# Diagonals of B through DRAM and the skip term on TensorE, in the scan part of a two-layer kernel

## The chip, the cores and the metric

The kernel runs on one core of one Trainium2 chip, in one launch, in float32. The metric is device time in microseconds (us) of the execution. The median of three runs is 18559.42 us (18539.3 to 18562.05).

## The reference

The input x is (8, 128, 128, 128): 8 images of 128 channels. Two layers are applied, each to the group-normalised x, with a residual. Layer 0 mixes a Fourier branch, a channel attention and grouped convolutions; the change doesn't touch it. Layer 1 is a selective scan over the pixels of an image, seen as a sequence of 16,384 tokens. Cut to what matters:

```python
xs, z = split(u @ W_in)                          # 256 + 256 channels
xc = silu(causal_conv4(xs) + conv_b)
dt, Bm, Cm = split(xc @ W_xproj)                 # 8, 16, 16
delta = softplus(dt @ W_dt + b_dt)
# for every token t, channel d (256), state n (16):
h[d, n] = exp(delta[d] * A[d, n]) * h[d, n] + delta[d] * xc[d] * Bm[n]
y[d] = sum_n h[d, n] * Cm[n]
y = (y + xc * D_param) * silu(z)                 # skip term, gate
out = y @ W_out
```

## The kernel before, in words

Parts a to d make layer 0 and write the image x1 to DRAM (X1). The last part, "e", is the scan, lines 1017 to 1390. Nearly all its engine instructions are issued through a helper, InOrder (line 180), which keeps each engine's instructions in program order; so the profile gives them line 180, and they are told apart by their tiles. DMAs on SP aren't held in that order: the scheduler places them.

The tokens are cut into 256 chunks of T = 512 (32 per image). A chunk is worked in 16 steps (ST). A step n has a half h of the channels, a pair mp of state indices and a k, and covers 128 partitions (32 channels x 4 state groups) and two state indices:

- **decay** (ACT): dA = exp(dlrep * A), two 128x512 activations, issued three steps ahead (LEAD). dlrep is delta spread over the partitions; it goes to DRAM (dld) and comes back by four DMAs per half.
- **product** (PE): hb, the term delta * xc * B, 32 matmuls of 64 rows by 32 columns, one step ahead. The moving operand, bd, holds B on the diagonal of 64x64 blocks; the stationary one, duT, is the transposed delta * xc. So the matmul with a diagonal broadcasts B over channels. hb has two PSUM buffers of two banks each.
- **scan** (DVE): two tensor_tensor_scan, reading dA from SBUF and hb from PSUM, writing hs.
- **weigh** (POOL): hc = hs * C (crep, from DRAM by DMA: cd, then four DMAs per pair).
- **add** (PE): matmuls with a 0/1 matrix (gath) that sum hc into y in PSUM, for one half of the channels over 8 steps.
- **keep_state** (ACT): the last column of hs is kept for the next chunk.

Beside this, the list `beside` says which other work is issued at which of the 16 steps, and for which chunk relative to the present one: norm of the input (u<-xin), the convolution as four matmuls per half (e_xc), its activation (xc), the gate (e_z, sz), xproj (e_x, dbl), step_sizes (e_dt) and its softplus (dl), drive on POOL (du = dl * xc), its transposes (e_t, duT), turn_b (four transposes of B, e_bt), keep_b (bt, a copy of B to SBUF), the final projection (e_o) and the residual.

What the change touches:

- **diagonals** (DVE) and **more_diagonals** (ACT): bd is made from a constant (same) and the transposed B. Pair mp = 0 takes four DVE products, pair 1 two DVE products and 16 small ACT activations, spread over steps 11 to 15 and 0 to 1.
- **skip** (DVE, steps 11 and 3): yt = xc * D_param + y, reading y from PSUM. **gated** (POOL, steps 12 and 4): yt = yt * sz.
- **step_sizes_act** (step 7): softplus, dld to DRAM, the four dlrep loads of half 0, the four crep loads of pair 1, the four dlrep loads of half 1.
- Buffers: xin 2, xc 3, bd 2, dlrep 2, crep 3. The four tags bank0 to bank3 are one PSUM bank each: bank1 is shared by half 1 of e_xc, e_z and e_dt and by e_t and e_o; bank2 is e_bt's and bank3 is y's.

Every DMA of SP and ACT takes the next of eight semaphores in turn and so waits until the DMA eight before it has landed.

## Time and profile before

| | us |
|---|---|
| median of three runs | 18559.42 |
| profiled execution, its own time | 18481.4 |
| its span, first to last instruction | 18479.6 |
| scan part: first and last scan start | 6617.5 and 18451.9 |
| busy over the span: PE, DVE, ACT, POOL | 16503.3, 14244.2, 12009.6, 13090.9 |
| mean granted TensorE clock | 0.958 |

| scan part, mean of one (ns) | |
|---|---|
| scan hs, DVE, 128x512, with state | 1269 |
| hc product, POOL, 128x1024 | 2377 |
| dA activation, ACT, 128x512 | 714 |
| table load, ACT | 1283 |
| residual acc, DVE, 128x512 | 1156 |

How to read it: busy time is the union of an engine's instruction spans. Ends of matmuls are modelled, and matmuls overlap, so the distance from one group's start to the next one's says more of the pace than a mean. A wait is put down to the event that came last. "issue" stands for a wait in which nothing that the profile shows was missing. Idle time of an engine that is not the bound costs nothing. The scan part is periodic, so it is read per chunk, from a window in its middle.

### The profile page before, as it was taken

Reading aid. Unit: us, or ns where it says so; the run is one execution under the profiler, and the core shown is the slowest. Engines: PE = TensorE matmul, PEld = TensorE weight load, DVE = VectorE, ACT = ScalarE, POOL = GpSimd, SP = SyncE. Lnnn points to the kernel's source line nnn. Section 1 sums busy time; section 2 is a strip of 40 time slices with the busy share of each in tenths; the row PEclk is TensorE's granted clock in tenths of the full one; section 3 lists DMA queues with packets and bytes.
Section 4 is the critical chain, followed back from the end, with each engine's and each line's share of the span. In section 5 each row is a group of like instructions: output and inputs, shape, how many; then the busy total and the mean of one; then the engine's idle time right before and its main releaser. Section 6 shows DMA issues by size and latency. Waiting matters only on the chain.

```text
span 18479.6 us, 790974 instructions
## 1 busy us (share of the span) xinstructions
PE 16503.3 (89%) x353336; PEld 9529.9 (52%) x353336; DVE 14244.2 (77%) x15987; ACT 12009.6 (65%) x26077; POOL 13090.9 (71%) x7572
## 2 busy tenths in 40 slices
PE   7789988888888889999999999999999999999998
PEld 5566665566555544444444444444444444444444
DVE  5544544334444479999999999999999999999999
ACT  4443434334233358778778878888888878887887
POOL 3333334444222269999999999999999989998998
PEclk8889999988999999999999999999999999999999
DMA  9963337777776654444454445444544454445443
GB/s 375 371 235 89 96 106 248 240 230 218 207 204 192 186 139 100 103 96 100 97 105 101 100 96 108 99 99 98 106 98 99 100 103 100 99 98 105 98 98 88
DMA packets 2434566, 2601.34 MB, mean 141 GB/s; under 512 B 1221965, under 2 KB 1624013, under 8 KB 2396866
## 3 DMA queue, kind: packets, MB, share of 16 engines
q1 hardware_dynamic: 1730850, 2206.28, 43.9%
q10 hardware_dynamic: 679840, 277.32, 7.1%
q0 software_dynamic: 20480, 67.13, 1.1%
q8 instruction: 2783, 45.60, 1.1%
q14 instruction: 613, 5.02, 0.1%
HBM read 1715.23 MB, written 834.93 MB: 138 GB/s over the span
## 4 chain that ended last, share of the span: by engine, by line
PE 56%; DVE 22%; DMA 8%; issue 7%; ACT 6%; POOL 1%; SPq 1%; DVEq 0%; ACTq 0%; POOLq 0%
DVE hs L180 15%; PE hb L180 14%; PE y L180 8%; PE c_mm L180 6%; PE e_xc L180 4%; DVE bd L180 3%; PE e_z L180 3%; PE e_x L180 3%; PE d_b L180 2%; PE a_mm L180 2%; DMA d_of<-OFL 2%; PE c_gram L180 2%; PE d_p L180 2%; DMA X<-d_x 2%; ACT L180 2%
## 5 line engine op out<-in xcount | busy, mean ns | idle before, releaser
L180 POOL TENSOR_TENSOR hc<-hs,crep 128x1024 f32<-128x1024 f32 x4096 | 9653.4, 2377 | 982.4 <-DVE hs L180 858.1
L180 DVE TENSOR_TENSOR_SCAN hs<-dA,state,hb 128x512 f32<-128x512 f32 x7936 | 9611.4, 1269 | 558.2 <-PE hb L180 418.8
L180 PEld LDWEIGHTS hb<-bd,duT 64*32 64x32 f32 x262144 | 3727.5, 106 | 3971.3 <-issue 2808.4
L180 PE MATMUL hb<-bd,duT 64*32 64x128 f32 x262144 | 4919.3, 275 | 798.9 <-issue 417.8
L180 ACT ACTIVATE dA<-dlrep,A 128x512 f32<-128x512 f32 x8192 | 5443.8, 714 | 59.6 <-DMA dlrep<-dld 51.6
L180 PE MATMUL e_xc<-u,wf 128*128 128x512 f32 x4096 | 2263.9, 646 | 34.1 <-DVE A L1046 20.8
L180 PE MATMUL y<-hc,gath 128*32 128x512 f32 x16384 | 2053.4, 601 | 32.5 <-issue 31.2
L180 ACT COPY state<-hs 128x2 f32<-128x2 f32 x4096 | 775.9, 189 | 1676.2 <-DVE hs L180 1649.5
L180 ACT ACT_TABLE_LOAD x1057 | 1356.1, 1283 | 75.0 <-PE e_dt L180 40.1
L180 PE MATMUL c_mm<-src,taps 32*32 32x512 f32 x32768 | 1211.5, 626 | 191.8 <-issue 158.7
L180 DVE COPY vst<-c_mm 128x512 f32<-128x512 f32 x1024 | 685.0, 689 | 717.4 <-PE c_mm L180 620.6
L180 ACT ACTIVATE bd<-same,bt 128x64 f32<-128x64 f32 x4096 | 1054.0, 339 | 0.8 <-PE hb L180 0.8
L180 DVE TENSOR_TENSOR bd<-same,e_bt 128x512 f32<-128x512 f32 x1536 | 1036.7, 675 | 0.0
L180 PEld LDWEIGHTS c_mm<-src,taps 32*32 32x32 f32 x32768 | 681.2, 105 | 683.7 <-issue 493.5
L180 POOL TENSOR_SCALAR qm<-vst,cst 128x512 f32<-128x512 f32 x256 | 505.4, 2070 | 745.4 <-DVE vst L180 745.2
L180 ACT ACTIVATE junk<-vst 128x256 f32<-128x256 f32 x1024 | 416.4, 410 | 923.0 <-DVE vst L180 921.9
L180 PE MATMUL a_mm<-xt,wp 128*128 128x256 f32 x3072 | 760.6, 409 | 264.5 <-ACT pk L180 184.1
L180 POOL TENSOR_TENSOR eo<-eo,et 128x1008 f32<-128x1008 f32 x128 | 298.8, 2334 | 969.3 <-DVE et L180 960.8
L180 POOL DMA_DIRECT2D X<-d_x x256 | 139.1, 543 | 1069.5 <-DVE d_x L180 939.9
L180 PEld LDWEIGHTS e_xc<-u,wf 128*128 128x128 f32 x4096 | 654.7, 194 | 440.2 <-issue 436.1
L180 DVE TENSOR_TENSOR d_x<-d_p,d_x 128x512 f32<-128x512 f32 x256 | 274.9, 1074 | 780.3 <-DMA d_x<-in_x 490.0
L180 PEld LDWEIGHTS a_mm<-xt,wp 128*128 128x128 f32 x3072 | 619.3, 205 | 421.7 <-ACT pk L180 194.6
(179 smaller groups left out, 20011.2 us busy)
## 6 DMA issues: line engine op xcount, KB each, us to landing
dlrep<-dld SPq DMA_DIRECT2D x2048, 256.0 KB
crep<-cd SPq DMA_DIRECT2D x2048, 128.0 KB
dld<-dl SPq DMA_DIRECT2D x256, 512.0 KB
src<-Pq SPq DMA_DIRECT2D x128, 544.5 KB
src<-Pv SPq DMA_DIRECT2D x128, 544.5 KB
src<-Pk SPq DMA_DIRECT2D x128, 544.5 KB
src<-Px SPq DMA_DIRECT2D x128, 544.5 KB
xt<-in_x SPq DMA_DIRECT2D x64, 1024.0 KB
```

Source lines behind the costliest of these rows:

```text
L180: made = method(*args, **kwargs)
```

## The change

bd is no longer computed. Four DRAM scratch tensors diag (two pairs mp, two parities of the chunk), each 128 x 2048, are filled with zeros once, before the scan. Per chunk, B transposed (e_bt) is copied to SBUF by ACT (bt), and four small DMAs write its values to the diagonal places of the two scratch tensors of the chunk's parity: 64 partitions x 16 places x 2 values, so 1,024 pieces of 8 bytes each. Everything off the diagonal stays zero. Then each scratch tensor is loaded whole, 1 MB, into bd (now three buffers). turn_b moves from step 7 to step 6, ahead of step_sizes, and keep_b from step 8 (DVE) to step 6 (ACT).

In program order the bd loads stand between the two halves of dlrep. As scheduled, SP's order in a chunk is: xin, cd (2), crep of pair 0 (4), diag (4), dld, bd of pair 0, dlrep of half 0 (4), bd of pair 1, crep of pair 1 (4), dlrep of half 1 (4): 26 DMAs, against 20 before. Before, the order was cd, xin, crep, dld, dlrep, crep, dlrep.

The skip term becomes a matmul of xc with a diagonal matrix dd (D_param on its diagonal), which opens y's accumulation group, at step 5 for half 0 and at step 14 for half 1. The gate becomes one DVE product, y (PSUM) times sz, at steps 11 and 3; POOL has no part of it any more. xin goes to one buffer, xc to two. The weights wf are loaded and folded earlier, in a pool of their own.

```diff
+    cp = ctx.enter_context(tc.tile_pool(name="e_c", bufs=1))
+    DROW = NTB * NQ * ND * 2
+    diag = {(n, mp): dram.tile([128, DROW], F32, name=f"diag{n}{mp}") for n in range(2) for mp in range(2)}
+        zero = zp.tile([128, DROW], F32, name="zero")
+        nc.gpsimd.memset(zero, 0.0)
+        for d in diag.values():
+            nc.sync.dma_start(d, zero)
...
+        dd = cp.tile([128, 2, 128], F32, name="dd")
+        for h in range(2):
+            nc.vector.tensor_scalar(dd[:, h, :], unit, d_par[:, h : h + 1], None, ALU.mult)
...
-            xin = wk.tile([128, T], F32, name="xin")
+            xin = wk.tile([128, T], F32, name="xin", bufs=1)
...
-            c["xc"] = wk.tile([128, 2, T], F32, name="xc", bufs=3)
+            c["xc"] = wk.tile([128, 2, T], F32, name="xc", bufs=2)
...
                 if h:
+                    load_b(i, 0)
+                    load_b(i, 1)
                     repeat_c(i, 1)
...
         def keep_b(i):
             c = ch[i]
-            c["bt"] = wk.tile([128, NTB, DS], F32, name="bt")
-            dve.tensor_copy(c["bt"], c["bp"][:, : NTB * 32].rearrange("p (j n) -> p j n", n=32)[:, :, :DS])
-        def diagonals(i, mp, j):
...
-        def more_diagonals(i, which):
...
+            bt = wk.tile([128, NTB, DS], F32, name="bt")
+            act.copy(bt, c.pop("bp")[:, : NTB * 32].rearrange("p (j n) -> p j n", n=32)[:, :, :DS])
+            for mp in range(2):
+                d = diag[i % 2, mp]
+                for x in range(2):
+                    ap = [[DROW + 2, ND], [2 * ND, NTB * NQ], [1, 2]]
+                    to = bass.AP(d.tensor, d.offset + x * ND * DROW, ap)
+                    frm = bt[ND * x : ND * x + ND].rearrange("p j (q m) -> p (j q) m", m=NM)[:, :, 2 * mp : 2 * mp + 2]
+                    nc.sync.dma_start(to, frm)
+        def load_b(i, mp):
+            t = ch[i]["bd", mp] = wk.tile([128, NTB, NQ, ND, 2], F32, name="bd", bufs=3)
+            nc.sync.dma_start(t.rearrange("p j q t m -> p (j q t m)"), diag[i % 2, mp])
...
                 ch[i]["y", g // 2] = bank("y", 3)
+                pe.matmul(ch[i]["y", g // 2], lhsT=dd[:, g // 2, :], rhs=ch[i]["xc"][:, g // 2, :], start=True, stop=False, skip_group_check=True)
...
-        def skip(i, h):
+        def gated(i, h):
...
-            dve.scalar_tensor_tensor(
-                c["yt"][:, h, :], c["xc"][:, h, :], d_par[:, h : h + 1], c.pop(("y", h)), ALU.mult, ALU.add
-            )
-        def gated(i, h):
-            yt = ch[i]["yt"][:, h, :]
-            gps.tensor_tensor(yt, yt, ch[i]["sz"][:, h, :], ALU.mult)
+            dve.tensor_tensor(c["yt"][:, h, :], c.pop(("y", h)), c["sz"][:, h, :], ALU.mult)
...
-            (3, -1, lambda i: skip(i, 1)),
-            (4, -1, lambda i: gated(i, 1)),
+            (3, -1, lambda i: gated(i, 1)),
+            (6, 1, turn_b),
             (6, 1, step_sizes),
+            (6, 1, keep_b),
-            (7, 1, turn_b),
-            (8, 1, keep_b),
-            (11, 0, lambda i: skip(i, 0)),
+            (11, 0, lambda i: gated(i, 0)),
-            (12, 0, lambda i: gated(i, 0)),
```

More of the change, by code (lines that the diff above doesn't have):

```diff
@@ L158, in _layout @@
         o["wdt"][32 * h : 32 * h + DR] = a[p + "W_dt"][:, h * 128 : (h + 1) * 128]
-    o["same64"] = np.tile(np.eye(64, dtype=np.float32), (2, 1))
     o["gath"] = np.tile(np.eye(32, dtype=np.float32), (4, 1))
@@ L1024, in tile_kernel @@
     QR = 32
-    with tc.tile_pool(name="e_c", bufs=1) as cp, tc.tile_pool(name="e_w", bufs=2) as wk, tc.tile_pool(
+    cp = ctx.enter_context(tc.tile_pool(name="e_c", bufs=1))
+    wf = cp.tile([128, 4, DI], F32, name="wf")
+    nc.sync.dma_start(wf.rearrange("p a d -> p (a d)"), I["cw"].partition_broadcast(128))
+    DROW = NTB * NQ * ND * 2
+    diag = {(n, mp): dram.tile([128, DROW], F32, name=f"diag{n}{mp}") for n in range(2) for mp in range(2)}
+    with tc.tile_pool(name="e_0", bufs=1) as zp:
+        win_x = zp.tile([128, DI], F32, name="win_x")
+        nc.sync.dma_start(win_x, I["win"][:, 0:DI])
+        for k in range(4):
+            nc.vector.tensor_tensor(wf[:, k, :], wf[:, k, :], win_x, ALU.mult)
+        zero = zp.tile([128, DROW], F32, name="zero")
+        nc.gpsimd.memset(zero, 0.0)
+        for d in diag.values():
+            nc.sync.dma_start(d, zero)
+    with tc.tile_pool(name="e_w", bufs=2) as wk, tc.tile_pool(
         name="e_h", bufs=4
@@ L1035, in tile_kernel @@
         gath = fixed("gath", [128, NR], I["gath"])
-        same = fixed("same", [128, ND], I["same64"])
         unit = fixed("unit", [128, 128], I["consts"][:, 0:128])
-        win = fixed("win", [128, 2 * DI], I["win"])
+        win = fixed("win", [128, DI], I["win"][:, DI : 2 * DI])
         wx = fixed("wx", [128, 2, 128], I["wx"])
@@ L1046, in tile_kernel @@
         nc.vector.tensor_scalar(A, A, -1.0, None, ALU.mult)
-        wf = cp.tile([128, 4, DI], F32, name="wf")
-        nc.sync.dma_start(wf.rearrange("p a d -> p (a d)"), I["cw"].partition_broadcast(128))
-        for k in range(4):
-            nc.vector.tensor_tensor(wf[:, k, :], wf[:, k, :], win[:, 0:DI], ALU.mult)
         state = cp.tile([128, NM, NBK], F32, name="state")
@@ L1115, in gate @@
                 ps = bank("e_z", h)
-                pe.matmul(ps, lhsT=win[:, DI + h * 128 : DI + (h + 1) * 128], rhs=c["u"][:, 3:], start=True, stop=True)
+                pe.matmul(ps, lhsT=win[:, h * 128 : (h + 1) * 128], rhs=c["u"][:, 3:], start=True, stop=True)
                 act.activation(c["sz"][:, h, :], ps, AF.Silu)
@@ L1194, in keep_b @@
             c = ch[i]
-            c["bt"] = wk.tile([128, NTB, DS], F32, name="bt")
-            dve.tensor_copy(c["bt"], c["bp"][:, : NTB * 32].rearrange("p (j n) -> p j n", n=32)[:, :, :DS])
-        def diagonals(i, mp, j):
-            c = ch[i]
-            if (mp, j) in ((0, 0), (1, 0)):
-                c["bd", mp] = wk.tile([128, NTB, NQ, ND, 2], F32, name="bd")
-            to = [128, NQ, ND, 2]
-            b = c["bp"][:, 32 * j : 32 * j + DS].rearrange("p (q m) -> p q m", m=NM)[:, :, 2 * mp : 2 * mp + 2]
-            dve.tensor_tensor(
-                c["bd", mp][:, j], same.unsqueeze(1).unsqueeze(3).to_broadcast(to), b.unsqueeze(2).to_broadcast(to), ALU.mult
-            )
-        def more_diagonals(i, which):
-            c = ch[i]
-            for n in which:
-                j, q, m = 2 + n // 8, n // 2 % 4, n % 2
-                at = NM * q + 2 + m
-                act.activation(c["bd", 1][:, j, q, :, m], same, AF.Identity, scale=c["bt"][:, j, at : at + 1])
+            bt = wk.tile([128, NTB, DS], F32, name="bt")
[10 more added lines that the diff above has]
+            nc.sync.dma_start(t.rearrange("p j q t m -> p (j q t m)"), diag[i % 2, mp])
         ST = 16
@@ L1280, in add @@
                         ch[i]["y", g // 2][k * NR : (k + 1) * NR, :], lhsT=gath, rhs=hcs[ST * i + 4 * g + k][:, j, :],
-                        start=(g % 2 == 0 and j == 0), stop=(g % 2 == 1 and j == 1), skip_group_check=True,
+                        start=False, stop=(g % 2 == 1 and j == 1), skip_group_check=True,
                     )
@@ L1292, in skip @@
                 c["yt"] = wk.tile([128, 2, T], F32, name="yt", bufs=1)
-            dve.scalar_tensor_tensor(
-                c["yt"][:, h, :], c["xc"][:, h, :], d_par[:, h : h + 1], c.pop(("y", h)), ALU.mult, ALU.add
-            )
-        def gated(i, h):
-            yt = ch[i]["yt"][:, h, :]
-            gps.tensor_tensor(yt, yt, ch[i]["sz"][:, h, :], ALU.mult)
+            dve.tensor_tensor(c["yt"][:, h, :], c.pop(("y", h)), c["sz"][:, h, :], ALU.mult)
         def project(i):
@@ L1320, in tile_kernel @@
             (0, 1, lambda i: conv(i, 1, 2)),
-            (0, 0, lambda i: diagonals(i, 1, 1)),
-            (0, 0, lambda i: more_diagonals(i, range(6, 11))),
             (1, 1, lambda i: conv(i, 1, 3)),
-            (1, 0, lambda i: more_diagonals(i, range(11, 16))),
             (2, 1, conv_act),
             (2, -1, lambda i: add(i, 3, 0, 1)),
-            (3, -1, lambda i: skip(i, 1)),
-            (4, -1, lambda i: gated(i, 1)),
+            (3, -1, lambda i: gated(i, 1)),
             (4, 1, xproj),
@@ L1342, in tile_kernel @@
             (10, 0, lambda i: add(i, 1, 0, 1)),
-            (11, 0, lambda i: skip(i, 0)),
-            (11, 1, lambda i: diagonals(i, 0, 0)),
+            (11, 0, lambda i: gated(i, 0)),
             (11, 1, lambda i: turn(i, 0)),
             (11, 2, lambda i: conv(i, 0, 1)),
-            (12, 0, lambda i: gated(i, 0)),
             (12, 1, lambda i: turn_act(i, 0)),
-            (12, 1, lambda i: diagonals(i, 0, 1)),
             (12, 2, lambda i: conv(i, 0, 2)),
-            (13, 1, lambda i: diagonals(i, 0, 2)),
             (13, 1, lambda i: turn(i, 1)),
@@ L1354, in tile_kernel @@
             (14, 1, lambda i: turn_act(i, 1)),
-            (14, 1, lambda i: diagonals(i, 0, 3)),
             (14, 0, lambda i: add(i, 2, 0, 1)),
-            (15, 1, lambda i: diagonals(i, 1, 0)),
-            (15, 1, lambda i: more_diagonals(i, range(6))),
             (15, 2, lambda i: conv(i, 1, 0, 1)),
```

## The prediction

> **What bounds the kernel now.** I read the slices first: the change touches only the scan part, from about 6,560 us to the end.

> ```profile
> PE   7789988888888889999999999999999999999998
> DVE  5544544334444479999999999999999999999999
> POOL 3333334444222269999999999999999989998998
> DMA  9963337777776654444454445444544454445443
> ```

> From slice 15 on PE, DVE and POOL are all at 9 and the DMA engines at 4 to 5: a balanced pipeline, whose sum must be made per chunk. I took the window 9,000 to 18,000 us; 195 chunks start in it (the copy into bt occurs 195 times), 46.15 us each, and there are 256 chunks (512 half-chunks of x, 8,192 scans). The busy times in that window:

> ```profile
> 9000.00:18000.00 9000.00, 8288.41 (x220210) 4311.17 (x220210) 8541.06 (x8173) 7233.77 (x15359) 8259.17 (x3899) 0.99 0.45 101
> ```

> Columns: length, PE, weight loads, DVE, ACT, POOL, granted clock, DMA share, GB/s. Divided by 195: PE 42.5 us of a chunk, DVE 43.8, ACT 37.1, POOL 42.4. So DVE is ahead by 1.3 us only. The groups that the change touches, and what PE waits for, in the same window:

> ```profile
> L180 DVE TENSOR_TENSOR bd<-same,e_bt 128x512 f32<-128x512 f32 x1168 | 789.0, 675 | 0.0
> L180 ACT ACTIVATE bd<-same,bt 128x64 f32<-128x64 f32 x3104 | 798.7, 339 | 0.8 <-PE hb L180 0.8
> L180 DVE SCALAR_TENSOR_TENSOR yt<-xc,dv,y 128x512 f32<-128x512 f32 x389 | 284.5, 731 | 6.4 <-PE y L180 6.3
> L180 POOL TENSOR_TENSOR yt<-yt,sz 128x512 f32<-128x512 f32 x389 | 497.6, 1279 | 0.0
> ```

> ```profile
> PE hb L180 <- issue: 324.9, 223, 4.4
> PE hb L180 <- DVE hs L180: 265.0, 416, 1.2
> PE e_o L180 <- ACT dl L180: 82.0, 172, 0.5
> PE y L180 <- issue: 22.2, 16, 2.8
> PE e_xc L180 <- issue: 9.6, 6, 2.1
> ```

> PE's account closes: 8288.4 busy + 356.7 waiting for nothing shown + 265.0 for DVE + 82.0 for ACT = 8992 of 9000 us. Per chunk: 42.5 + 1.83 + 1.36 + 0.42. DVE's lead costs PE only 1.36 us a chunk. That is what relieving DVE can return, unless it also shortens PE's own work.

> **The change, part by part, per chunk.**

> *Diagonals off DVE and ACT.* DVE loses 6 x 0.675 = 4.05 us and the bt copy, 0.20; ACT loses 16 x 0.256 (798.7 / 3104) = 4.1 and takes the copy, about 0.2. With skip and gate fused into one DVE product instead of the scalar_tensor_tensor (0.731; I take the 0.675 of the equally large product that also reads PSUM), DVE goes to 43.8 - 4.05 - 0.20 - 0.1 = 39.4, ACT to 33. POOL loses two 1.279 us products: 39.8. All three fall well below PE.

> *Skip on PE.* Two full 128x128 matmuls of 512 columns are added, one at step 5, one at step 14. The pace of such a pair of matmuls, PE's timeline:

> ```profile
> 12040.86 1.99 PE L180 MATMUL e_z<-u,win 128*128 128x512 f32 x4
> 12042.77 1.16 PE L180 MATMUL hb<-bd,duT 64*32 64x128 f32 x64
> 12043.86 1.98 PE L180 MATMUL e_x<-xc,wx 128*128 128x512 f32 x4
> 12045.78 1.16 PE L180 MATMUL hb<-bd,duT 64*32 64x128 f32 x64
> ```

> Two matmuls (four records) hold PE 1.91 us from their start to the next start, so each 0.95: **+1.9 to 2.0 us**, all on PE; nothing hides it, since the sum above leaves PE no idle time but what DVE gave it.

> *turn_b before step_sizes.* PE waits 0.42 us a chunk for dl before e_o. The four e_bt transposes (0.36 us from first to next start) stood between e_dt and e_o and covered part of it; now they stand ahead of e_dt. The table load and the two softplus behind e_dt stay as long. **+0.36**. If ACT's freed 4 us brings the table load forward, it is 0: I keep 0 to 0.36 and take the larger, because the chain starts at e_dt's end, which ACT cannot advance.

> *DVE wait returned.* Between 0 and -1.36. With DVE at 39.4 little is left, but in steps 7 to 13 DVE has 7 scan pairs, the residual and a gate (about 18.3 us at 2.38 a pair, from six scans in 7.14 us) against some 16.3 us on PE, with one hb buffer of slack. I take **-1.2**.

> *New waits that cost nothing.* The bt copy on ACT waits for e_bt, which PE ends before e_dt; behind it stand the norm of u and the softplus, which wait for later things anyway, so they lose its 0.2 us at most, out of 9 idle. xc with two buffers: its last reader is now the skip matmul at step 14 of its own chunk, done before the next conv_act but one. xin with one buffer: its load goes out after the norm that reads the old one, a chunk ahead of need.

> *Transfers.* New per chunk: 4 scattering DMAs of 1,024 pieces of 8 bytes, and two loads of 1 MB. No row shows an 8-byte write to DRAM. Nearest is the store out<-acc, 128-byte pieces, in the DMA view of 9,000 to 9,925 us:

> ```profile
> q10 hardware_dynamic: 32800, 4.19, 3.6%
> ```

> 0.036 x 16 x 925 us / 32,800 = 16.2 ns a piece. 4,096 x 16.2 / 16 engines = 4.1 us. Far ends: 8 ns (half of that row, were cost to fall with bytes): 2.1 us; 28 ns (queue 10 between 1,400 and 2,500 us, 15.3% of 16 engines for 95,680 packets of 504 bytes on average): 7.2 us. The loads: xt<-in_x has the same 128x2048 shape and the first 1,400 us move 324 GB/s on the mean, so 3.2 us each. DMA share goes from 0.45 to about (20.8 + 4.1 + 6.5) / 46.15 = 0.68. Bandwidth suffices; order and latency decide, as rival 2 prices.

> [...]

> *PE's waits for nothing shown*, 1.83 us a chunk, fall inside products, and they thicken where the DMA engines are jammed: in 12,217 to 12,231 us, a burst of 128-byte loads, PE lost 4.1 us in 14; in 12,031 to 12,045 us, with the engines idle, none after the first 0.2 us. More transfers mean more of it: between 0 and 1.83 x 0.23 / 0.45 = 0.9. I take **+0.3**, since most of the new bytes are long packets. [...]

> *Prologue.* 4 MB of zeros (13 us at 324 GB/s) go out before the scan; now an acc load holds SP 11.73 us there. 0 to +13 once; I take 0.

> **Sum:** 1.95 + 0.36 - 1.2 + 0.3 = +1.4, rounded up to 1.5 a chunk for the acc and out chunks, where these terms meet a jam; 256 x 1.5 = **+384 us**. The profiled execution ran 18481.4 us (span 18479.6), 78 us below the median 18559.42; I add the difference to the median: **18,940 us**.

> **Rivals.**

> 1. *Forecast: PE becomes the bound, DVE's and POOL's relief is idle time.* 18,940. For: PE's closed account. Chance 0.45.

> 2. *The transfer path binds.* On SP, bd0 is issued behind dld and ahead of dlrep0, and waits for the scatter to land; dlrep0, bd1, crep1 and dlrep1 queue behind it. In one chunk of SP's timeline:

> ```profile
> 12007.53 1.71 SPq L1140 DMA_DIRECT2D crep<-cd  x4
> 12009.33 0.38 SPq L1155 DMA_DIRECT2D dld<-dl  x1
> 12014.23 2.44 SPq L1161 DMA_DIRECT2D dlrep<-dld  x4
> ```

> crep's data end at about 12,011.5; scatter +4.1; dld +2; bd0 +3.2; dlrep0 +4.2: landed at 12,025.5, where decay used it at 12,021.8. Second duT, behind two decays on ACT (1.24 + 0.2 + 1.24 + 0.56), is ready at 12,028.8; product(0) started at 12,027.7 before, and about 1 us later with the step-14 skip ahead of it. So it is about even at 4.1 us of scatter; each further microsecond costs about one per chunk. At 7.2 us: +3.1, with rival 1's sum +4.6 a chunk, or 19,740. At 2.1 nothing. Chance 0.25.

> 3. *Faster: PE isn't as full as its busy time says.* Ends of matmuls are modelled. Adding the shortest start-to-start distances of PE's groups in this part (product 1.08, two adds 1.85, e_z 1.91, a conv tap 0.95 to 1.06, and so on) gives about 41.1 us, 1.4 below busy. Then PE needs 41.1 + 1.95 + 0.78 + 1.83 = 45.7, -0.45 a chunk or 18,440 in all, and if half of the waits in products fall into other waits, 44.8: 18,200. It decides if over 1 us of PE's busy time is slack that DVE imposed. Against: the clock dips that lengthen matmuls are in the busy time too, and remain. Chance 0.20; the first of the two is the likelier, 18,440.

> 4. *About even*, within 0.2% (what a measurement of this kernel can tell from no change), gains and terms cancelling: 0.10. That the change does not do what it says is excluded by the built order: the 6 products and 16 activations are gone, two matmuls y<-xc,dd are there.

> **Numbers.** Faster by over 0.2%: 0.20 (rival 3). Same: 0.10. Slower: 0.70 (1 and 2). Range: 18,400 (near the middle of rival 3) to 19,600 (most of rival 2).

> **What would show it.** Right: DVE near 0.85 busy, ACT and POOL lower, PE's wait for DVE near 0 and its share above 0.93; e_o's wait near 0.8 us a chunk. Rival 2: decays waiting for dlrep, or products for duT or bd loads. Wrong: a chunk shorter than 46 us.

## The result and the profile after

The changed kernel takes 19902.72 us (median of 4 runs, 19885.01 to 19934.7) against 18549.36 us for the kernel before (4 runs on the same chip): **a ratio of 1.0734, 95% interval 1.0714 to 1.0754, slower**. The sign was the forecast's; the size, 18,940 us in a range of 18,400 to 19,600, was not. The profiled execution took 19934.7 us, its span is 19932.9 us; it was the longest of the four, and the profiled one of before (18481.4 us) is shorter than all four of before, so the two profiles differ by more (5.71 us in a chunk of the scan part) than the medians do (1353 us, or 5.3 for each of the 256 chunks).

The slices of the page of after, the same four engines as shown of before:

```profile
PE   6789988888888788888888888888888888888888
DVE  5544543434444677777777777777777787777777
POOL 3333344442222577777777777777777777777777
DMA  9953357777766667666676666766666666666665
```

DVE and POOL fell from 9 to 7, as forecast. But PE fell too, from 9 to 8, although it was given more to do, and the DMA engines rose from 4 or 5 to 6. An engine that is the bound and loses share is waiting. The window of exactly 160 chunks in the middle of the scan part (51.96 us each), and PE's waits in it (the helper is line 179 here):

```profile
9915.54:18229.89 8314.35, 7360.13 (x181762) 3679.10 (x181760) 6512.11 (x5602) 5319.91 (x10235) 6413.24 (x2886) 0.96 0.64 130
```

```profile
PE hb L179 <- issue: 602.9, 409, 5.1
PE e_o L179 <- ACT dl L179: 150.9, 141, 1.1
PE hb L179 <- ACT duT L179: 115.5, 42, 8.0
PE y L179 <- issue: 41.5, 25, 4.5
PE e_xc L179 <- issue: 34.2, 25, 3.3
PE hb L179 <- DVE hs L179: 3.9, 10, 0.6
```

The wait for DVE is gone (3.9 us of 8,314). In its place stands "issue", waits in which nothing that the profile shows was missing: 409 of them in products alone, up to 5.1 us long. The granted clock fell from 0.99 to 0.96. The same account for each run, all over 160 chunks, in us per chunk:

| run | chunk | PE busy | issue | hs (DVE) | dl | duT | half clock | DMA full |
|---|---|---|---|---|---|---|---|---|
| before | 46.25 | 42.59 | 1.83 | 1.37 | 0.42 | 0.01 | 1.30 | 17.3% |
| after | 51.96 | 46.00 | 4.24 | 0.02 | 0.94 | 0.72 | 4.12 | 42.8% |
| x1 diagonals alone | 50.71 | 44.26 | 4.43 | 0.06 | 0.87 | 0.99 | 5.42 | 41.9% |
| x2 skip alone | 47.14 | 44.37 | 1.45 | 1.13 | 0.00 | 0 | 0.79 | 17.3% |
| x3 dlrep first | 51.09 | 45.61 | 4.08 | 0.10 | 0.97 | 0.01 | 3.80 | 37.1% |
| x4 dead copies | 47.83 | 43.45 | 2.96 | 0.98 | 0.41 | 0 | 2.88 | 27.4% |
| x5 no loads | 48.04 | 44.51 | 2.26 | 0.03 | 1.03 | 0.16 | 1.13 | 28.3% |
| x6 no scatter | 48.83 | 44.71 | 3.08 | 0.01 | 0.98 | 0 | 2.67 | 26.2% |
| x7 other scratch | 51.23 | 45.80 | 4.23 | 0.03 | 0.96 | 0.17 | 3.88 | 38.2% |
| x9 few pieces | 50.90 | 45.47 | 4.35 | 0.01 | 0.95 | 0.08 | 4.35 | 37.6% |
| x12 few, other scratch | 50.08 | 45.23 | 3.79 | 0.01 | 0.95 | 0.06 | 3.48 | 32.3% |
| x8 scatter by ACT | 54.38 | 46.67 | 3.36 | 0 | 4.33 | 0.01 | 7.64 | 33.6% |

The columns issue, hs, dl and duT are PE's waits: for nothing shown, for the scan, for the softplus, and for the transposed delta * xc. "Half clock" is the time per chunk in which the trace's clock record stands at 0.5; it holds only 1.0 and 0.5. "DMA full" is the share of the scan part in which the 16 DMA engines, by their packets, were over 95% busy (means over 3 us; how a packet is assigned to them moves the figure by a point or two).

After less before is 5.71 us: **issue +2.41, a lower clock +1.4, skip +2.0, duT +0.71, dl +0.52, DVE -1.35**. Skip and clock are told apart by the run with the skip alone: PE busy +1.78 there, while 0.51 us less of the time ran at half clock, which is worth an estimated 0.25 (by the record's 0.5, half of it); so the skip is 2.03, and what is left of PE's +3.41 is 1.38. In after the same estimate gives as much: 2.82 us more per chunk at half clock lose 1.41. As a price it is rough: in x6, x9 and x8, where it gives 0.68, 1.52 and 3.17 us over before, PE busy less the skip rose by 0.09, 0.85 and 2.05.

**What "issue" is.** The page has a DMA queue named instruction; of before and of after:

```profile
q8 instruction: 2783, 45.60, 1.1%
```

```profile
q8 instruction: 2791, 45.73, 1.0%
```

Each packet is 16 KB. 2,783 packets times 256 are 712,448; PE's records in the trace are 712,449. In after it is 714,496 and 714,499. So the queue brings PE's instructions, 256 to a packet. Of the 318 waits on PE put down to issue in the scan part of before, 317 fall into the same sixteenth of that count modulo 256, so at one place of a block; in after 641 of 714. PE goes on 1.4 to 1.5 us (median) after the packet has landed. By these counts the waits are late instruction fetches. The packet's own time hardly grows (median 1.07 us with the DMA engines under 10% busy, 1.27 us with full ones, in after), so most of the lateness lies ahead of its start. One of them in after, with the windows around it:

```profile
12019.68 1.16 PE L179 MATMUL hb<-bd,duT 64*32 64x128 f32 x64
12023.60 2.08 PE L179 MATMUL e_xc<-u,wf 128*128 128x512 f32 x2 [2.76 <-issue]
12025.61 1.96 PE L179 MATMUL hb<-bd,duT 64*32 64x128 f32 x64
12027.50 2.07 PE L179 MATMUL e_xc<-u,wf 128*128 128x512 f32 x2
```

```profile
12000.00:12014.00 14.00, 13.92 (x362) 7.36 (x366) 14.00 (x13) 7.57 (x18) 13.93 (x8) 1.00 1.02 250
12014.00:12024.00 10.00, 6.20 (x149) 3.08 (x139) 6.53 (x6) 7.04 (x17) 6.89 (x4) 0.94 0.93 208
12024.00:12030.00 6.00, 6.00 (x104) 2.61 (x106) 2.22 (x2) 3.27 (x5) 1.96 (x1) 0.54 0.02 4
12030.00:12044.00 14.00, 14.00 (x352) 6.66 (x337) 11.61 (x11) 8.71 (x17) 11.05 (x5) 1.00 0.03 6
```

In the first 14 us the DMA engines were full (1.02 by their packets' starts) and PE lost almost nothing, 0.08 us: full engines didn't make every fetch late at once here. In the next 10 us, with the engines at 0.93, PE worked 6.2 us (the gap of 2.76 is one fetch, one of 1.04 ahead of it another). Then the clock fell to 0.54 for 6 us, and the same groups took 2.08 and 1.96 us in place of 1.13 and 1.16: a busy PE, taking 1.7 to 1.8 times as long. With the engines at 0.03 and the clock at 1.00 it was busy 14 us of 14. The second cost followed the first: the clock record, which has two values, 0.5 and 1.0, stands at 0.5 from 12,022.73 to 12,029.56, so from 1.9 us into the gap of 2.76, with the gap of 1.04 begun some 7 us ahead. The spells at 0.5 last 4.0 us on the mean in before and 4.6 in after (3.5 to 4.8 in nearly all runs). What came ahead of this one is usual: ahead of the 234 half-clock spells in the scan part of after, PE had been idle for 2.6 us of the last 7 (median; the longest single gap in them 2.4), against 0.5 us ahead of a random point; over all sixteen profiles the medians are 2.2 to 2.9 and 0 to 0.5.

### The profile page after: what moved, and what is told of

The parts are those of the page before. It is cut to its first block, busy times and chain, and to the rows that moved or that the text cites. A ratio compares the mean times of both kernels' runs of the same rounds, so it can differ in the third digit from the quotient of the medians.

```text
span 19932.9 us, 789132 instructions
## 1 busy us (share of the span) xinstructions
PE 17351.5 (87%) x354360; PEld 9736.7 (49%) x354360; DVE 13421.1 (67%) x14197; ACT 11003.0 (55%) x22237; POOL 12482.4 (63%) x7061
## 4 chain that ended last, share of the span: by engine, by line
PE 70%; DMA 11%; issue 7%; ACT 6%; DVE 4%; SPq 1%; POOL 1%; ACTq 0%; POOLq 0%; DVEq 0%; another core or an unknown queue 0%
PE hb L179 19%; PE y L179 12%; PE e_xc L179 9%; PE c_mm L179 6%; DMA dlrep<-dld 3%; PE e_z L179 2%; PE e_x L179 2%; DMA dld<-dl 2%; DMA d_of<-OFL 2%; PE d_b L179 2%; PE e_o L179 2%; PE a_mm L179 2%; ACT L179 2%; PE d_p L179 2%; PE c_gram L179 2%
## 5 line engine op out<-in xcount | busy, mean ns | idle before, releaser
L179 PE MATMUL hb<-bd,duT 64*32 64x128 f32 x262144 | 5092.0, 278 | 1186.2 <-issue 955.9
L179 PEld LDWEIGHTS hb<-bd,duT 64*32 64x32 f32 x262144 | 3803.9, 107 | 4542.8 <-issue 3436.4
L179 PE MATMUL e_xc<-u,wf 128*128 128x512 f32 x4096 | 2324.9, 662 | 81.1 <-issue 61.9
L179 PE MATMUL y<-hc,gath 128*32 128x512 f32 x16384 | 2186.5, 627 | 66.0 <-issue 64.5
L179 PEld LDWEIGHTS y<-hc,gath 128*32 128x32 f32 x16384 | 433.4, 112 | 1219.8 <-issue 1200.0
L179 PE MATMUL e_o<-yt,wout 128*128 128x512 f32 x1024 | 529.9, 642 | 243.8 <-ACT dl L179 243.8
```

Of the source, the lines that this page charges most:

```text
L179: made = method(*args, **kwargs)
```

## The experiments

Three theories at first: late instruction fetches under the transfers; the path scatter, bd, dlrep (rival 2); TensorE's own added work (rival 1).

**x1, the diagonals through DRAM alone**: the change without its skip and gate parts; xc has three buffers again, and dA has 9 in place of 10. Against after, cut:

```diff
-                pe.matmul(ch[i]["y", g // 2], lhsT=dd[:, g // 2, :], rhs=ch[i]["xc"][:, g // 2, :], start=True, stop=False, skip_group_check=True)
...
-            (3, -1, lambda i: gated(i, 1)),
+            (3, -1, lambda i: skip(i, 1)),
+            (4, -1, lambda i: gated(i, 1)),
```

> The changed kernel with the old skip on VectorE and the old gate on GpSimd: diagonals through DRAM alone (xc with three buffers again, and dA with nine instead of ten to make room). Per chunk of the scan part, TensorE's account was 42.5 us busy + 1.83 waiting for nothing shown + 1.36 for VectorE + 0.42 for dl before, and 46.0 + 4.27 + 0.03 + 0.94, and 0.73 for duT, after. Fetch theory (long full stretches of the DMA engines delay TensorE's instruction blocks, and the clock falls after such a stop): the waits for nothing shown stay near 4.3 and the clock at 0.96, some 49.5 us a chunk, ratio 1.04 to 1.05 to before. Path theory (dlrep lands late behind the bd load): dA's wait for dlrep stays near 6 us a chunk, duT's near 0.7, ratio about 1.02. TensorE-work theory (skip matmuls and the moved transposes are the loss): within 0.99 to 1.01.

Measured: 19559.23 us, ratio 1.0597 (1.0569 to 1.0624). Most of the loss is here, with not one matmul added. Issue 4.43 and half clock 5.42 us per chunk. It is more than any of the theories had said; the fetch theory, with 1.04 to 1.05, was the nearest.

**x2, the skip and the gate alone**: before, with `dd`, the opening matmul and the fused gate:

```diff
+                pe.matmul(ch[i]["y", g // 2], lhsT=dd[:, g // 2, :], rhs=ch[i]["xc"][:, g // 2, :], start=True, stop=False, skip_group_check=True)
...
-            (3, -1, lambda i: skip(i, 1)),
-            (4, -1, lambda i: gated(i, 1)),
+            (3, -1, lambda i: gated(i, 1)),
```

> The kernel before with the skip term on TensorE and the gate as one VectorE product; diagonals as before. Two matmuls a chunk: 433 us in 173 chunks after, 2.5 us with the lowered clock, 1.9 to 2.0 at full clock; VectorE's 1.36 us of lead can hide part. Fetch theory: no transfers added, so waits for nothing shown stay at 1.8 and the clock at 0.98 to 0.99; 0.7 to 1.5 us a chunk longer, ratio 1.01 to 1.02. Path theory: the same. TensorE-work theory: most of the loss, ratio 1.05 or more.

Measured: 18694.73 us, ratio 1.012 (1.0097 to 1.0143), where the theories of the fetch and of the path had it. Its waits:

```profile
PE hb L180 <- issue: 212.4, 171, 3.6
PE hb L180 <- DVE hs L180: 180.4, 292, 1.2
```

Two microseconds of matmuls cost 0.9 us of a chunk: the wait for dl vanished (0.4 us in 160 chunks), that for hs shrank, and so did issue.

**x3, dlrep of half 0 ahead of the bd loads on SP**:

```diff
+                    last = nc.sync.dma_start(t[q * NR : (q + 1) * NR], d[h].rearrange("(k r) t -> r k t", r=NR))
...
+            tc.add_manual_dep(made.ins, last.ins.name, after, reason="in order")
```

> The changed kernel with the load of bd for pair 0 issued behind the four dlrep loads of half 0 instead of ahead of them; bytes and instructions are the same. Path theory: dA's wait for dlrep falls from 6.6 us a chunk below 3, duT's and the late scans' go, 1.5 to 3 us a chunk back, ratio to before 1.03 to 1.05. Fetch theory: the waits for nothing shown stay near 4.3 us, ratio 1.06 to 1.075. TensorE-work theory: no change from 1.073.

Measured: 19722.42 us, ratio 1.0679 (1.0654 to 1.0704), inside the fetch theory's range. The wait for duT (0.72) is gone, 0.27 for bd itself came up. So rival 2's mechanism is real and worth under 1 us of the 5.7: 0.87 by the profiled chunks, 0.4 by the ratios (0.0055 of some 18,500 us, over 256 chunks).

**x4, before plus two copies of 1 MB per chunk, whose data nothing uses**, behind the last dlrep load:

```diff
+                made = nc.sync.dma_start(dead[n][:, 0:2048], X1[i % B, :, 2048 * n : 2048 * n + 2048])
```

> The kernel before, with two copies of 1 MB a chunk from DRAM to DRAM in rows of 8 KB, issued behind the last dlrep load of a chunk; nothing reads them. Fetch theory: the waits for nothing shown rise from 1.83 to between 2.5 and 4 us a chunk, the clock falls a little, ratio 1.01 to 1.04. Path theory: the copies stand where nothing waits for 20 us, so 1.00. TensorE-work theory: 1.00.

Measured: 18839.68 us, ratio 1.0202 (1.0184 to 1.022). Of before, in its 160 chunks, and of x4:

```profile
PE hb L180 <- issue: 264.6, 186, 4.4
```

```profile
PE hb L180 <- issue: 425.4, 289, 3.6
PE hb L180 <- DVE hs L180: 156.5, 244, 1.9
```

No instruction of PE, DVE, ACT or POOL changed, and nothing waits for the copies' data, yet PE's issue waits in products went from 264.6 us in 160 chunks of before to 425.4, and half clock from 1.30 to 2.88 us per chunk. Bytes alone slow this kernel: the chunk's +1.58 us is issue +1.13 and PE busy +0.86 at unchanged instructions, less 0.39 of the wait for the scan. This run carries the fetch theory.

**x5, no loads**, and **x6, no scatter**: after, with the first or the second of these edits:

```diff
+            if i > 0:
+                ch[i]["bd", mp] = ch[i - 1]["bd", mp]
+                return
```

```diff
-                    nc.sync.dma_start(to, frm)
+                    if i < 2:
+                        nc.sync.dma_start(to, frm)
```

> The kernel after, with bd loaded for the first chunk only; the later chunks use that bd, so the right B is left out of the products. The scatter of 4,096 pieces of 8 bytes per chunk goes on, and PE's instructions are the same. Theory of the long loads (the 2 MB per chunk of bd delay PE's instruction fetch): PE's waits for nothing shown fall from 4.27 us per chunk to between 1.8 and 2.3, the half-clock share of the time from 8.1 % to about 3 to 4 %, the extra wait for duT (0.73) and part of that for dl go; what is left is the skip, +2.3, dl +0.3, less the DVE wait of 1.3: +1.3 to +1.9 us per chunk, ratio 1.018 to 1.03. Rival, theory of the small pieces (4,096 descriptors per chunk hold the fetch up): the waits stay at about 4 us and the ratio at 1.055 to 1.07. Rival, TensorE's own extra work sets the time: 1.06 or more.

> The kernel after, with the scatter done for the first two chunks only; the two loads of 1 MB per chunk go on from the scratch as it then stands, so the right B is left out of the products of later chunks. Theory of the long loads: PE's waits for nothing shown stay at 4.0 to 4.4 us per chunk, the half-clock share at 7 to 9 %, and the ratio at 1.06 to 1.073; only the wait for duT (0.73) may go, since the loads no longer wait for the scatter to land. Theory of the small pieces: waits fall to 1.8 to 2.5, ratio 1.02 to 1.035.

Measured: x5 18957.46 us, ratio 1.0233 (1.0205 to 1.0262), as the theory of the long loads said. x6 19147.82 us, ratio 1.034 (1.0308 to 1.0372): neither theory is borne out whole, since the ratio is at the upper end of what the theory of the small pieces had (1.02 to 1.035), and the issue wait, 3.08, lies above its 1.8 to 2.5 and below the other's 4.0 to 4.4. The loads cost something by themselves. The scatter by itself costs less (x5 is 0.90 us above the skip alone: dl +1.03, issue +0.81, duT +0.16, hs -1.10), yet taking it away gives back 3.1 us. So it acts mostly together with the loads. Two things differ in x6: the scatter is missing, and with it SP's order. In after, bd stands ahead of dlrep; in x6 behind it, in each half. SP's own timeline, of after and then of x6:

```profile
12045.31 1.71 SPq L1153 DMA_DIRECT2D crep<-cd  x4
12047.12 3.58 SPq L1220 DMA_DIRECT2D diag<-bt  x4
12050.81 0.60 SPq L1168 DMA_DIRECT2D dld<-dl  x1
12052.90 0.34 SPq L1224 DMA_DIRECT2D bd<-diag  x1
```

```profile
12034.32 2.35 SPq L1153 DMA_DIRECT2D crep<-cd  x4
12038.17 0.38 SPq L1168 DMA_DIRECT2D dld<-dl  x1
...
12041.17 2.47 SPq L1176 DMA_DIRECT2D dlrep<-dld  x4
12045.02 0.34 SPq L1225 DMA_DIRECT2D bd<-diag  x1
```

The scatter holds SP for 3.58 us ahead of dld. The next four runs take it apart.

**x7, the scatter to a second set of scratch**, so that no load waits for it; SP's order becomes that of x6:

```diff
-                d = diag[i % 2, mp]
+                d = diag[i % 2 + 2 * (i > 1), mp]
```

> The kernel after, but from the third chunk on the scatter writes to a second set of scratch tensors, and the loads go on reading the first set, which keeps the B of the first two chunks; the right B is left out of the products. All transfers stay, only the wait of a bd load for the scatter of its own chunk is gone. The scatter and the loads cost more together (after 51.96 us per chunk, against 47.14 with the skip alone) than each by itself (48.04 without the loads, 48.83 without the scatter): 2.2 us are left over. Theory of the wait: bd of pair 0 holds SP until the scatter has landed, and what queues behind it then goes out in one jam; without it the chunk falls to 49 to 50 us, ratio 1.04 to 1.05. Rival, theory of the pieces and their issue: the four issues of the scatter on SP and its 4,096 pieces are what makes the other transfers late and slow; the chunk stays at 51 to 52 us, ratio 1.06 to 1.073.

Measured: 19727.83 us, ratio 1.0681 (1.0665 to 1.0697), 51.23 us per chunk, as the rival had it: the theory of the wait fell. Wait and order together are 0.73 us by the profiled chunks (0.4 by the ratios); x3 had returned as much by the order alone, with the wait in place.

**x8, the scatter issued by ACT**:

```diff
-                    nc.sync.dma_start(to, frm)
+                    nc.scalar.dma_start(to, frm)
```

> The kernel after, with the four DMAs of the scatter issued by ScalarE in place of SyncE. The bytes, the pieces and the wait of the bd loads for them stay; SP no longer spends 3.6 us per chunk on issuing the scatter, and ScalarE, which is idle for some 18 us of a chunk, does. Theory of SP's queue: dld and dlrep go out some 3 us sooner, the decays' wait for dlrep (6.6 us per chunk) falls by 3 us or more, the wait for duT (0.72) goes, and the jam is shorter; chunk 49.5 to 51 us, ratio 1.045 to 1.06. Rival, theory of the wait or of the pieces: the jam stays as it is, 51.3 to 52.5 us, ratio 1.065 to 1.08.

Measured: 20549.65 us, ratio 1.1126 (1.111 to 1.1143), worse than either theory. PE's first two waits, and ACT's own:

```profile
PE e_o L179 <- ACT dl L179: 693.2, 160, 8.5
PE hb L179 <- issue: 491.7, 297, 4.1
```

```profile
ACT u L179 <- issue: 480.0, 150, 9.2
```

The issue holds ACT for 3 us per chunk (480.0 / 160), right behind bt and ahead of the softplus, for which e_o waits: dl went from 0.94 to 4.33. ACT's idle time was elsewhere. Yet issue fell from 4.24 to 3.36, duT to 0.01, and the decays' wait for dlrep from 6.6 us per chunk to 2.6. So the issuing on SP does matter. And the half clock rose to 7.64 us with fewer late fetches: here too it went with PE's idle time (7.7 us per chunk), though most of that was the wait for dl.

**x9, 64 pieces per scatter DMA in place of 1,024**, and **x12**, x9 and x7 together:

```diff
-                    nc.sync.dma_start(to, frm)
+                    k = NTB * NQ if i < 2 else 1
+                    ap[1] = [2 * ND, k]
+                    nc.sync.dma_start(bass.AP(d.tensor, d.offset + x * ND * DROW, ap), frm[:, :k])
```

> The kernel after, but from the third chunk on each of the four scatter DMAs writes only the first of its 16 places, so 64 pieces of 8 bytes in place of 1,024; B of the other places stays that of the first two chunks, so the right B is left out of the products. The four issues on SP and the wait of the bd loads for them stay. Theory of the queue (four more DMAs on SP, ahead of dld, whatever they carry, delay it and pack what follows): the chunk stays within 1 us of the kernel after, 51 to 52 us, ratio 1.06 to 1.073, and the decays' wait for dlrep stays at 5 us or more per chunk. Theory of the pieces (4,096 small writes hold the DMA engines up): the chunk falls to 48.8 to 49.8 us, close to the run without the scatter (48.83), ratio 1.034 to 1.048, and the wait for dlrep to 2 us or less.

> The two cuts of the runs x7 and x9 together: from the third chunk on the four scatter DMAs write 64 pieces each in place of 1,024, and to a second set of scratch tensors, so that no load waits for them; the right B is left out of the products. Against the run without the scatter (x6, 48.83 us per chunk, whose DMAs stand in the same order on SP) only the four issues with their 256 pieces are more. If pieces, order and issues simply add (x9 says 1.06 us for the pieces, x7 0.73 us for the order and the wait, 1.34 us of the 3.13 are then left for the issues): 50.2 us per chunk, 49.9 to 50.5, ratio 1.052 to 1.058. Theory that the issues cost nothing by themselves and only the pieces and the order count: 48.8 to 49.3 us, ratio 1.034 to 1.04.

Measured: x9 19644.44 us, ratio 1.0631 (1.0614 to 1.0649), 50.90 us; x12 19425.02 us, ratio 1.0518 (1.0491 to 1.0546), 50.08 us per chunk where adding up had said 50.2. Neither theory of x9 is borne out whole: the ratio is in the range of the theory of the queue, while the decays' wait for dlrep, 4.0 us per chunk, lies between the 5 of the one and the 2 of the other. By the profiled chunks the parts add up, and the way from before to after is, per chunk:

| step | profiled chunks | us | us by the ratios |
|---|---|---|---|
| skip and gate | before 46.25 to x2 47.14 | +0.89 | +0.87 |
| loads of 2 MB, turn_b ahead, less work on DVE and ACT | to x6 48.83 | +1.69 | +1.59 |
| four scatter issues on SP, 64 pieces each | to x12 50.08 | +1.25 | +1.29 |
| the other 3,840 pieces | to x7 51.23 | +1.15 | +1.18 |
| wait of bd for the scatter, and bd ahead of dlrep | to after 51.96 | +0.73 | +0.38 |

The last column takes the ratios of the medians, each to before on the same chip, times 18,500 us / 256. It agrees but for the last step, since the profiled execution of after is 32 us above its median and before took 18,549 us on its chip, 31 to 98 us more than on the others. By the ratios x12 also lies 0.4 us below what x7 and x9 add up to, so the sizes hold to about 0.4 us.

How can four issues of some 3 us in all on SP cost PE 1.25 us? They move dld, dlrep, bd and crep later and closer together. From x6 to x12 the decays' wait for dlrep went from 0.3 to 2.2 us per chunk and the share of time with full DMA engines from 26.2 to 32.3%; after has 42.8%. In after the late fetches stand there: 3.6 of its 4.2 us of issue fall into time with full engines (running means over 3 us), in before only 0.7 of 1.8. By these traces what counts is how long the engines have been full. The table has what PE lost to issue waits, per 100 us of such time:

| | before | x4 | x6 | x12 | after |
|---|---|---|---|---|---|
| first 2 us of a full stretch | 0.5 | 0.5 | 2.4 | 7.9 | 5.1 |
| beyond 4 us of a full stretch | 22 | 24 | 16 | 19 | 18 |
| engines under 10% busy | 2.2 | 2.1 | 1.2 | 1.0 | 0.9 |
| time beyond 4 us, us per chunk | 2.9 | 7.0 | 5.8 | 11.0 | 17.3 |

The rate beyond 4 us is much the same in these runs (15 to 24 in all runs of the first table); what grows is the time that is spent there, with long packets (x4) as with four small DMAs that pack the others (x12). That is read from the traces. No run tried the same bytes at another spacing with all else equal, and why a fetch starts late while the engines are full is not shown.

**z1, x4's copies as 8 x 16 rows of 8 KB**, to see whether certain DMA engines matter:

```diff
-                made = nc.sync.dma_start(dead[n][:, 0:2048], X1[i % B, :, 2048 * n : 2048 * n + 2048])
+                made = nc.sync.dma_start(
+                    dead[n][:, 0:2048].rearrange("(p a) t -> a p t", a=8),
+                    X1[i % B, :, 2048 * n : 2048 * n + 2048].rearrange("(p a) t -> a p t", a=8),
+                )
```

> The kernel before, plus two copies of 1 MB per chunk whose data nothing uses (as in x4_dead_copies, which lost 2.0 %), but with each copy laid out as 8 x 16 rows of 8 KB, so that it may be spread over fewer of the 16 DMA engines. It asks whether the delay of PE's instruction fetch is tied to certain DMA engines. If the instruction fetch uses engines that these copies leave alone: PE's waits for nothing shown near 1.8 us per chunk, ratio 1.00 to 1.007. If it uses the ones that they load: 3 us or more, ratio 1.02 to 1.04. If the copies are spread over all 16 as before: 2.7 to 3.2 us, ratio 1.016 to 1.024, and the question stays open.

Measured: 19047.14 us, ratio 1.0283 (1.0254 to 1.0312). Issue was 2.47 us, between the cases, and a wait for duT of 1.49 us, behind late dlrep loads, made up most of the loss. The question stays open.

**Three versions meant to beat the kernel before**: y1 moves one more group of diagonals to ACT, y2 and y3 are, in this order:

```diff
-    QR = 32
+    QR = 64
...
-            t = wk.tile([128, W, QR], F32, name="acc")
+            t = wk.tile([128, W, QR], F32, name="acc", bufs=1)
```

```diff
+            (6, 1, step_sizes),
             (6, 0, lambda i: add(i, 0, 1)),
-            (6, 1, step_sizes),
```

and of y1 the main lines:

```diff
-                j, q, m = 2 + n // 8, n // 2 % 4, n % 2
+                j, q, m = 1 + n // 8, n // 2 % 4, n % 2
...
-            (0, 0, lambda i: diagonals(i, 1, 1)),
-            (0, 0, lambda i: more_diagonals(i, range(6, 11))),
+            (0, 0, lambda i: more_diagonals(i, range(8, 16))),
```

> A way to take work off VectorE that adds no transfer: the kernel before, with one more group of the diagonals of pair 1 moved from VectorE to ScalarE (24 small activations and 5 VectorE products per chunk, in place of 16 and 6). VectorE loses 0.68 us per chunk, ScalarE gains 8 x 0.26 = 2.1 us, out of 9 us that it is idle. Fetch theory: no bytes are added, so PE's waits for nothing shown stay at 1.8 us, and the wait for hs (1.36 us per chunk) falls by 0.3 to 0.6; ratio 0.990 to 0.998. Rival: ScalarE's order makes decay or dl late; ratio 1.000 to 1.01.

> A version that may beat the kernel before: before, with the rows of the image loaded and stored 64 at a time in place of 32 (one buffer in place of two), so that the pieces of acc and out are 256 bytes in place of 128, and half as many. Fetch theory: the bursts of 128-byte pieces, in which PE's waits for nothing shown are thickest (two chunks in eight last 50.2 and 47.4 us in place of 44.6), shrink; ratio 0.990 to 0.997. Rival: a piece of 256 bytes takes twice as long, or with one buffer the load of the next rows waits for the store of the last and the residual waits for it: 1.000 to 1.01.

> A version that may beat the kernel before: before, with step_sizes put ahead of add(i, 0, 1) at step 6 instead of behind it. Two accumulating matmul groups of about 1.0 us in all then stand between e_dt and e_o on TensorE, and cover the wait of e_o for dl (0.42 us per chunk), as the skip matmul did in the run with the skip alone, where this wait was nil. No byte is added. If e_dt's operand dbl is ready by then: -0.3 to -0.45 us per chunk, ratio 0.990 to 0.994. Rival, dbl isn't ready or what PE gains goes into its wait for hs (1.37), since VectorE is 1.3 us from being the bound: 0.996 to 1.002.

Measured: y1 1.0018 (1.0007 to 1.003), y2 1.0057 (1.0041 to 1.0074), y3 1.0064 (1.0049 to 1.0079); none beats it; all three are as slow as their rivals had it, or (y3) slower. y1 took hs from 1.37 to 0.91 as expected, but xc became late on ACT (0.23) and issue was 2.00. y2 did lower issue, to 1.58, but dbl became late by 0.51 (10 waits, of up to 13.8 us, where SP held the load of the single acc buffer back for the store of the last rows), and hs rose to 1.46. In y3 the wait for dl went (0.42), and 0.25 for dbl and 0.11 more for hs came in; PE busy was 0.35 higher, with half clock at 1.90.

## Why the prediction was wrong

The step that failed is "*PE's waits for nothing shown*": "between 0 and 1.83 x 0.23 / 0.45 = 0.9. I take +0.3". Measured +2.41, outside its own bounds, and with it +1.4 through the clock, which the sum didn't have at all. I had the right row (4.1 us lost of 14 in a burst, none with idle engines) and scaled it wrongly: by the growth of the mean DMA share, and then down again because long packets looked harmless. The time with full engines rose from 8.0 to 22.2 us per chunk, 2.8 times, and the part of it beyond 4 us of a full stretch from 2.9 to 17.3, six times; x4 shows that long packets do it too. And it was named as waits, not as idle time, with which the half clock rose from 1.30 to 4.12 us per chunk. On the fetch itself, PE in after lost 0.9 us per 100 to issue waits with the DMA engines under 10% busy, and 18 once they had been full for over 4 us.

- *Skip on PE*, 1.95: 2.03, right. That it would come to the chunk undiminished was wrong: alone it costs 0.89, since other waits gave way.
- *turn_b ahead*, +0.36: +0.52, undersized. e_o waits up to 1.1 us for dl. x5, x6, x9 and x12 all have 0.95 to 1.03, so the transfers aren't the cause; what makes up the 0.16 beyond the forecast, no run separates.
- *DVE wait returned*, -1.2: -1.35, right, and DVE, ACT and POOL went to 40.7, 33.2 and 40.1 us per chunk against 39.4, 33 and 39.8 forecast. PE's share, which was to be above 0.93, is 0.885 (7360 of 8314): the forecast of PE as the bound saw its work, not its idle time.
- *Diagonals alone*: what the relief returned, 1.35, was spent several times over. x1 is the change with this part alone, and it is 6% slower.
- *Transfers*: 8-byte pieces took 7.7 ns each (1,048,576 packets in 256 chunks), not 16.2, just below the low end of 8; the scatter is 2.0 us of the 16 engines. The bd loads took 6.5 us per chunk (256 packets of 406 ns on 16 engines), as forecast. The DMA share is 0.64, against 0.68. All of this was near or cheaper, and the time still came out above rival 2's 19,740, which is why bytes and shares weren't the right measure.
- *Rival 2* gave the nearest time, 19,740, and not the cause: decays did come to wait for dlrep, as it said,

```profile
L179 ACT ACTIVATE dA<-dlrep,A 128x512 f32<-128x512 f32 x5120 | 3397.7, 714 | 1062.0 <-DMA dlrep<-dld 1057.6 <-ACT state L179 0.5
```

  6.6 us per chunk, against 33.4 us in the whole 9,000 us window of before. But ACT has slack; only 0.72 reached PE through duT. And it happened at a scatter price at which the prediction had rival 2 cost nothing, since SP's 3.58 us of issuing weren't in its chain. (That chain's own terms add up to 12,025.0, not 12,025.5, and 7 scan pairs, the residual and a gate to 18.5 us, not 18.3; neither moves the forecast.)
- *Rival 3* (faster) fell: x2, which adds nothing but the skip to PE, is 1.2% slower.

## What to carry to other kernels

Here a bound engine needed its instructions as well as its data. Where waits "for nothing shown" sit at a fixed count of instructions (641 of 714 at one place of 256 in after), look at how long all DMA engines are full at a stretch (beyond 4 us PE lost 18 us per 100 in after), and price a new transfer by that, also when nobody waits for its data (x4 lost 2.0%). Add to it what the clock takes when TensorE has been made idle (2.82 us more per chunk at half clock in after). And count the issuing of a DMA as time of the queue that issues it, in the chain of whatever stands behind it there: some 3 us of small scatter DMAs cost 1.25 us per chunk on SP by packing what follows (x6 to x12), and on a ScalarE idle for a third of the time they raised the wait for dl by 3.39 us per chunk (x8) by standing ahead of its softplus.
